# Masking whole key tiles through the bias of the exponents instead of through a matrix product

## The chip, the cores and the metric

The kernel runs on one core of a Trainium2 chip. The metric is the device time of one execution in microseconds (us), the median of three runs. A core has a matrix engine (TensorE, PE in the profile, with its weight loads shown as PEld), three engines for elementwise work (VectorE or DVE, ScalarE or ACT, GpSimd or POOL), and SyncE (SP), which here only issues DMAs. The engines run side by side, each through its own instructions in order, and wait for each other through semaphores. Products land in PSUM, everything else lies in SBUF.

## The reference

Two stages over a batch of 4 sequences of 512 tokens, 128 features each. The first stage, where the change lies, is full attention with 16 heads of 64:

```
x1 = x + attention(layernorm(x))
scores = (q @ k.T) / 8 ;  scores += -50 * (key is later than query)
out = softmax(scores) @ v ;  attention = out @ Wr
```

The mask is a penalty of -50 and no exclusion: a later key keeps its exponent, smaller by exp(-50). The second stage is six layers of local attention and feed-forward on layernorm(x1); the change does not touch it.

## The kernel before

In the first stage a piece of work is a `Rows` object: one sequence `b`, one pair of heads `c` (8 pairs) and one tile `t` of 128 queries (4 tiles), 128 pieces in all. Each does this:

- `scores` (L250): four products, two key halves of 256 for each of two heads, into a PSUM tile `sc` of 128 x 2 x 512. There are two such tiles, so a piece reuses the tile of the piece two before it.
- `penalty` (L263): for each head, a bf16 product of a 128 x 128 identity with `pen`, added onto `sc` from column t*128 to the end, which is 512, 384, 256 or 128 columns for t = 0, 1, 2, 3. `pen` holds -50 where column > row: within the query's own tile it is a triangle, and over all the tiles behind it is the constant -50.
- `maximum` (L275, VectorE): the negated maximum `nm` over all 512 keys for both heads.
- `exponents` (L281, ScalarE): one exponent per head over 512 columns, with `nm` as the bias, and the sum of the row into `den` as a by-product, which the profile shows as a second, short instruction.
- `inverse` (L290, VectorE), `normalise` (L293, GpSimd): 1/den, and its product with the whole tile `pr` of exponents (three buffers).
- `transposes` (L304): eight TensorE transposes into two PSUM banks `pt`, copied into `pT` by ScalarE for the first head (L308) and by VectorE for the second (L310).
- `times_v1` (L321), two slots later, multiplies by v; VectorE copies the result out (L331).

The order is written out by hand: no scheduler moves anything. A loop over `m` makes 64 slots of two pieces, `now[0]` and `now[1]`. **Even slots** hold the query tiles 0 and 1, **odd slots** 2 and 3. TensorE's order in a slot is: `times_v1` of an older pair, scores of both pieces, penalties of both, a product for v (`make_v`, odd slots) or a step of a layernorm (some even slots), transposes of the previous slot's first piece (`old[0]`), one of `make_q` (even) or `make_k` (odd), transposes of `old[1]`. The product bank `ps_pj` that `make_q`, `make_k`, `make_v` and the layernorms use exists once. ScalarE's order in a slot is: copy of `old[0]`, two exponents of `now[0]`, copy of q (L216, even slots), copy of `old[1]`, two exponents of `now[1]`. VectorE's is: maximum of `now[0]`, copy of v (L236, odd slots), copy of `old[0]`, maximum of `now[1]`, copy of k (L222, odd slots), inverse of `now[0]`, copy of `old[1]`, inverse of `now[1]`. A layernorm's first step puts a subtraction (L95) and a square on VectorE and ScalarE ahead of the copies, in six of the even slots; its second step includes a reciprocal root (`rsqrt`, L79 to L85), most of which runs on GpSimd.

Of the kernel before, what the change touches and what calls it, by code (L numbers as in the profile page):

```python
# [8 lines left out]
F32 = mybir.dt.float32  # L9
BF16 = mybir.dt.bfloat16  # L10
I32 = mybir.dt.int32
AF = mybir.ActivationFunctionType
ALU = mybir.AluOpType
AX = mybir.AxisListType

P = 128
# [8 lines left out]
NW = P // W  # L25
EPS = 1e-5
NEG = -1e30
NVEC = 9


@with_exitstack
def body(ctx: ExitStack, tc: tile.TileContext, a, out: bass.AP):
# [5 lines left out]
    nc = tc.nc  # L38
    x = a["x"]
    B, S, _ = x.shape  # L40
    L = a["wqkv"].shape[0]
    NT = S // P
# [5 lines left out]
    small = ctx.enter_context(tc.tile_pool(name="small", bufs=4))  # L48
# [16 lines left out]
    ident16 = const.tile([P, P], BF16, tag="ident16", name="ident16")  # L65
    vecs = const.tile([P, L, NVEC], F32, tag="vecs", name="vecs")

# [73 lines left out]
    s1 = steps[0].enter_context(tc.tile_pool(name="s1", bufs=1))  # L141
# [26 lines left out]
    with tc.manual_schedule():  # L168
# [1 line left out]
        wk = s1.tile([P, INNER], F32, tag="wk", name="wk")  # L170
        wv = s1.tile([P, INNER], F32, tag="wv", name="wv")
        wr = s1c.tile([P, NC, EMB], F32, tag="wr", name="wr")
        pen = s1.tile([P, S], BF16, tag="pen", name="pen")
        xr = [s1.tile([P, NT, EMB], F32, tag="xr", name=f"xr{b}", bufs=2) for b in range(B)]
        for b in range(B):
            nc.sync.dma_start(out=xr[b], in_=x[b].rearrange("(t p) e -> p t e", p=P))
# [10 lines left out]
        def bank1():  # L187
            return ps1b.tile([P, 512], F32, tag="pj", name="ps_pj", bufs=1)
# [23 lines left out]
        def make_q(b, c):  # L212
            p = bank1()
            mm(p, lhsT=wq[:, c * P : (c + 1) * P], rhs=xnT[b], start=True, stop=True)
            q = qs[b, c] = s1.tile([P, S], F32, tag="q1", name="q1", bufs=2)
            nc.scalar.activation(q, p, AF.Copy, scale=0.125)  # L216

        def make_k(b, c):
            p = bank1()
            mm(p, lhsT=wk[:, c * P : (c + 1) * P], rhs=xnT[b], start=True, stop=True)  # L220
            k = ks[b, c] = s1.tile([P, S], F32, tag="k1", name="k1", bufs=2)
            nc.vector.tensor_copy(k, p)  # L222

        def make_v(b, j, t):

# [12 lines left out]
        class Rows:  # L238
# [19 lines left out]

            def penalty(self):

                sc, t = self.sc, self.t
                for h in range(2):
                    mm(  # L263
                        sc[:, h, t * P : S],
                        lhsT=ident16,
                        rhs=pen[:, 0 : S - t * P],
                        start=False,
                        stop=True,
                        skip_group_check=True,
                    )  # L270

            def maximum(self):
                sc = self.sc
                self.nm = small.tile([P, 2], F32, tag="nm", name="nm")
                nc.vector.tensor_reduce(self.nm, sc, AX.X, ALU.max, negate=True)  # L275

            def exponents(self):
                self.pr = s1.tile([P, 2, S], F32, tag="pr1", name="pr1", bufs=3)
                self.den = small.tile([P, 2], F32, tag="den", name="den")
                for h in range(2):  # L280
                    nc.scalar.activation(  # L281
                        self.pr[:, h, :],
                        self.sc[:, h, :],
                        AF.Exp,
                        bias=self.nm[:, h : h + 1],
                        accum_out=self.den[:, h : h + 1],
                    )

            def inverse(self):
                nc.vector.reciprocal(self.den, self.den)  # L290

            def normalise(self):
                nc.gpsimd.tensor_tensor(  # L293
                    self.pr, self.pr, self.den.unsqueeze(2).to_broadcast([P, 2, S]), ALU.mult
                )

            def transposes(self):
                b, c, t = self.b, self.c, self.t
                if t == 0:
                    pTs[b, c] = s1b.tile([P, 2, NT, S], F32, tag="pT1", name="pT1", bufs=2)  # L300
                for h in range(2):
                    pt = pt_bank()
                    for k in range(NT):
                        nc.tensor.transpose(pt[:, k * P : (k + 1) * P], self.pr[:, h, k * P : (k + 1) * P], ident)  # L304
                    dst = pTs[b, c][:, h, :, t * P : (t + 1) * P]
                    src = pt.rearrange("p (k q) -> p k q", k=NT)
                    if h == 0:
                        nc.scalar.copy(dst, src)  # L308
                    else:
                        nc.vector.tensor_copy(dst, src)  # L310

        def times_v1(b, c, half):

# [28 lines left out]
        mean, var, scale = norm_x(0)  # L342
# [4 lines left out]
        load_x(2)  # L347
        load_x(3)
        scale()
        make_q(0, 0)  # L350
        make_k(0, 0)


        last = len(rows) // 2
        for m in range(last + 1):
            b, c, odd = m // (2 * NC), m // 2 % NC, m % 2
            now = rows[2 * m : 2 * m + 2]
            old = rows[2 * m - 2 : 2 * m] if m else []
            if m >= 4:
                g = m // 2 - 2  # L360
                times_v1(g // NC, g % NC, odd)
            for r in now:
                r.scores()
            for r in now:
                r.penalty()
            if now:
                now[0].maximum()
            if m < 2:
                make_v(0, 0, 2 * m)
                make_v(0, 0, 2 * m + 1)  # L370
            if odd and c < NT:
                make_v(b, 1, c)
            elif odd and b + 1 < B:
                make_v(b + 1, 0, c - NT)
            if not odd and 1 <= c <= 3 and b + 1 < B:
                if c == 1:
                    norms[b + 1] = norm_x(b + 1)
                norms[b + 1][c - 1]()
            if b in range(1, B) and not odd and 4 <= c <= 6:
                norms1[b - 1][c - 4]()  # L380
            if old:
                old[0].transposes()
            if now:
                now[0].exponents()
                now[1].maximum()

            bn, cn = (b, c + 1) if c + 1 < NC else (b + 1, 0)
            if bn < B:
                (make_k if odd else make_q)(bn, cn)
            if now:  # L390
                now[0].inverse()
                now[0].normalise()
            if old:
                old[1].transposes()
            if now:
                now[1].exponents()
                now[1].inverse()
                now[1].normalise()
            if b > 0 and c == 1 and odd:
                y = bank1()  # L400
                project_out1(b - 1, y)
                residual1(b - 1, y)
                norms1[b - 1] = norm_x1(bank1, b - 1)
            if b == B - 1 and c == 2 and not odd:
                start = shifted(0), layer_tables(0)
# [379 lines left out]
    def slot(n, now, last):  # L785
# [15 lines left out]
        if u:  # L801
            exponents(u)
# [53 lines left out]
    with tc.manual_schedule():  # L856
# [4 lines left out]
        for n in range(-1, len(units) + NT + 3):  # L861
            if 1 <= n < 4:
                late[n - 1]()
            q = n // NT - 1
# [4 lines left out]
def _constants(n):  # L869

    import ml_dtypes
    import numpy as np

    f = np.float32
    half = np.arange(0, HD, 2, dtype=f)
    inv_freq = (f(1.0) / np.power(f(10000.0), half / f(HD))).astype(f)
    t = np.arange(n, dtype=f)
    freqs = (t[:, None] * inv_freq[None, :]).astype(f)
    base = ((half + f(0.4 * HD)) / f(1.4 * HD)).astype(f)
    power = (t - f(n // 2)) / f(W // 2)  # L880
    scale = np.power(base[None, :], power[:, None]).astype(f)
    cos, sin = np.cos(freqs), np.sin(freqs)
    inv = (f(1.0) / scale).astype(f)
    nt = n // P

    def by_token(lo, hi):
        return np.concatenate([lo, hi], 1).astype(f).reshape(nt, P, HD).transpose(1, 0, 2)


    tabs = np.stack(  # L890
        [
            by_token(cos * scale, cos * scale) * f(8.0),
            by_token(-sin * scale, sin * scale) * f(8.0),
            by_token(cos * inv, cos * inv),
            by_token(-sin * inv, sin * inv),
        ],
        axis=2,
    )

    q = np.arange(W)[:, None]  # L900
    k = np.arange(2 * W)[None, :] - W
    seen = (q >= k) & (q <= k + W)
    band = np.zeros((P, 2, 2 * W), f)
    for r in range(0, P, HD):
        band[r : r + W, 0] = np.where(seen & (k >= 0), 0.0, NEG)
        band[r : r + W, 1] = np.where(seen, 0.0, NEG)
    band = band.astype(ml_dtypes.bfloat16)

    pen = np.where(np.arange(n)[None, :] > np.arange(P)[:, None], -50.0, 0.0).astype(ml_dtypes.bfloat16)
    ident16 = np.eye(P).astype(ml_dtypes.bfloat16)  # L910
    return {"tabs": tabs, "band": band, "pen": pen, "ident16": ident16}

# [48 lines left out]
```

## Time and profile before

| | |
|---|---|
| median of three runs | 2291.53 us (2286.24 to 2292.44) |
| the profiled execution | 2288.88 us, of which the span of instructions is 2287.1 us |
| TensorE busy over the span | 2193.9 us, 96% |
| VectorE, ScalarE, GpSimd busy | 1684.3, 1299.6, 1453.9 us |
| first stage | from about 27 us (first scores) to about 562 us |
| granted TensorE clock | 0.996 of full |

A profile line gives an instruction group by its source line (L263), engine, operation, and the tiles out<-in. A timeline line begins with the start and the duration in us; "x16" says that 16 instructions were merged, and the bracket says how long the engine stood idle before it and what ended that. The end of a matmul is modelled and includes the time in which its result drains, so the distance between the starts of two groups tells more of TensorE than its busy time.

### The profile page before, as it was taken

What the parts mean: (1) busy time and instruction counts of PE and PEld (TensorE: products, weight loads), DVE (VectorE), ACT (ScalarE), POOL (GpSimd) and SP (SyncE); (2) the same over time, 40 slices, a digit from 0 to 9 for tenths busy, and PEclk for the clock granted to TensorE, in tenths of its full rate; (3) what the DMA queues carried; (4) which work ended last, traced back from release to release, by engine and by line L of the source; (5) the groups of instructions that cost most, each with busy time, mean ns of one, the idle gap of its engine ahead of it and who ended that gap; (6) DMA issues with size and microseconds to landing.
All of it is one profiled execution on the core that took longest, in us unless ns stands there. A gap on an engine that the chain in (4) does not pass through costs nothing.

```text
span 2287.1 us, 81570 instructions
## 1 busy us (share of the span) xinstructions
PE 2193.9 (96%) x35056; PEld 1445.6 (63%) x35088; DVE 1684.3 (74%) x2608; ACT 1299.6 (57%) x2166; POOL 1453.9 (64%) x1981
## 2 busy tenths in 40 slices
PE   6999999999999999999999999999999999999997
PEld 3555555555566666666666666666666666666664
DVE  3665656655778887788887888878888878888773
ACT  2554545544445666666666656566665666666562
POOL 1544545445777676777676777677766777766760
PEclk9999999999999999999999999999999999999998
DMA  3000000000322233222322323222332223222220
GB/s 117 1 1 1 1 1 1 1 1 1 75 62 68 62 87 74 64 69 68 88 69 61 75 66 94 63 64 68 85 83 61 68 63 87 76 66 71 65 56 15
DMA packets 91025, 125.81 MB, mean 55 GB/s; under 512 B 25262, under 2 KB 39468, under 8 KB 90668
## 3 DMA queue, kind: packets, MB, share of 16 engines
q1 hardware_dynamic: 90236, 119.02, 21.0%
q8 instruction: 279, 4.57, 0.9%
q10 hardware_dynamic: 432, 1.57, 0.2%
q14 instruction: 78, 0.64, 0.1%
HBM read 20.41 MB, written 1.05 MB: 9 GB/s over the span
## 4 chain that ended last, share of the span: by engine, by line
PE 84%; DVE 11%; issue 2%; ACT 1%; DMA 1%; POOL 0%; SPq 0%; POOLq 0%; ACTq 0%; DVEq 0%
PE ps_proj L459 19%; PE ps_one L567 13%; PE ps_one L662 7%; PE ps_att L637 6%; PE ps_att L605 6%; PE ps_sc L250 5%; PE ps_o L321 5%; PE ps_pt L304 4%; PE ps_proj L695 3%; PE ps_proj L696 3%; PE ps_proj L709 2%; DVE t L484 2%; DVE rot L480 2%; DVE yt L79 2%; PE ps_sc L263 2%
## 5 line engine op out<-in xcount | busy, mean ns | idle before, releaser
L495 POOL TENSOR_TENSOR rot<-rot,t 128x1024 f32<-128x1024 f32 x192 | 454.1, 2365 | 197.9 <-DVE t L484 195.3
L459 PE MATMUL ps_proj<-wqkv,xs 128*128 128x512 f32 x1152 | 554.5, 604 | 4.8 <-DVE t L484 3.2
L293 POOL TENSOR_TENSOR pr<-pr,den 128x1024 f32<-128x1024 f32 x128 | 240.8, 1894 | 270.9 <-DVE den L290 269.6
L470 ACT ACTIVATE sq<-ps_proj 128x1024 f32<-128x1024 f32 x192 | 196.9, 1026 | 358.7 <-PE ps_proj L459 305.8
L503 POOL TENSOR_TENSOR rot<-rot,ss 128x1024 f32<-128x1024 f32 x192 | 365.5, 1904 | 14.9
L459 PEld LDWEIGHTS ps_proj<-wqkv,xs 128*128 128x128 f32 x1152 | 198.4, 190 | 167.0 <-issue 146.8
L475 DVE TENSOR_REDUCE ss<-sq 128x16 f32<-128x1024 f32 x192 | 233.2, 1215 | 47.9 <-ACT sq L470 47.2
L275 DVE TENSOR_REDUCE nm<-ps_sc 128x2 f32<-128x1024 f32 x128 | 156.1, 1220 | 122.6 <-PE ps_sc L263 122.6
L480 DVE TENSOR_TENSOR rot<-ps_proj,lt 128x1024 f32<-128x1024 f32 x192 | 233.6, 1217 | 0.0
L484 DVE TENSOR_TENSOR t<-ps_proj,lt 128x1024 f32<-128x1024 f32 x192 | 233.1, 1214 | 0.4 <-POOL rot L495 0.4
L662 PEld LDWEIGHTS ps_one<-aT,wo 128*128 128x128 f32 x1536 | 187.0, 192 | 46.9 <-issue 46.2
L567 PE MATMUL ps_one<-ident,rot 128*128 128x128 f32 x1536 | 210.5, 280 | 4.7 <-issue 2.1
L308 ACT COPY pT<-ps_pt 128x512 f32<-128x512 f32 x128 | 75.1, 587 | 235.4 <-PE ps_pt L304 233.3
L82 POOL TENSOR_TENSOR yt<-y 128x32 f32<-128x32 f32 (+1 forms) x309 | 73.5, 238 | 209.6 <-DVE y L80 193.3
L615 DVE TENSOR_REDUCE mx<-ps_att 128x16 f32<-128x1024 f32 x96 | 117.5, 1224 | 101.6 <-PE ps_att L605 99.9
L662 PE MATMUL ps_one<-aT,wo 128*128 128x128 f32 x1536 | 187.9, 275 | 1.2 <-issue 0.9
L281 ACT ACTIVATE pr<-ps_sc,nm 128x512 f32<-128x512 f32 x256 | 175.1, 696 | 9.7 <-DVE nm L275 9.7
L567 PEld LDWEIGHTS ps_one<-ident,rot 128*128 128x128 f32 x1536 | 164.5, 141 | 24.0 <-issue 4.4
L637 PEld LDWEIGHTS ps_att<-vw,pT 64*32 64x32 f32 x9216 | 103.2, 105 | 93.2 <-ACT pT L570 53.7
L549 ACT COPY vt<-ps_proj 128x512 f32<-128x512 f32 x192 | 103.2, 590 | 93.9 <-PE ps_proj L459 92.3
L304 PEld LDWEIGHTS ps_pt<-ident,pr 128*128 128x128 f32 x1024 | 118.6, 142 | 55.9 <-issue 47.4
L637 PE MATMUL ps_att<-vw,pT 64*32 64x65 f32 x9216 | 128.9, 225 | 24.1 <-DVE t L484 14.5
(132 smaller groups left out, 3996.1 us busy)
## 6 DMA issues: line engine op xcount, KB each, us to landing
vw<-vt SPq DMA_DIRECT2D x1152, 65.0 KB, 2.1
vw_first<-vt SPq DMA_DIRECT2D x336, 65.0 KB, 2.0
wqkv<-in_wqkv_dram SPq DMA_DIRECT2D x18, 512.0 KB, 7.3
wo<-in_wo_dram SPq DMA_DIRECT2D x6, 512.0 KB
w<-in_w_dram SPq DMA_DIRECT2D x6, 341.0 KB, 4.0
xr<-in_x_dram SPq DMA_DIRECT2D x4, 256.0 KB, 5.6
out_dram<-tmp_t SPq DMA_DIRECT2D x4, 256.0 KB
w<-in_w_dram SPq DMA_DIRECT2D x12, 64.0 KB, 2.9
```

The costliest lines, as they stand in the source:

```text
L293: nc.gpsimd.tensor_tensor(self.pr, self.pr, self.den.unsqueeze(2).to_broadcast([P, 2, S]), ALU.mult)
L304: nc.tensor.transpose(pt[:, k * P : (k + 1) * P], self.pr[:, h, k * P : (k + 1) * P], ident)
L459: mm(p[:, c, :], lhsT=u.xs[:, u.T * P : (u.T + 1) * P], rhs=wpart[j][:, c * 512 : (c + 1) * 512], start=True, stop=True,)
L470: nc.scalar.activation(u.sq, u.p[j], AF.Square)
L475: nc.vector.tensor_reduce(u.ss[:, j * HEADS : (j + 1) * HEADS], heads(u.sq), AX.X, ALU.add)
L480: nc.vector.tensor_tensor(heads(t0), heads(pf), lt[:, u.T, 2 * j].unsqueeze(1).to_broadcast([P, HEADS, HD]), ALU.mult)
L484: nc.vector.tensor_tensor(t1.rearrange("p (h t d) -> p h t d", t=2, d=half), pf.rearrange("p (h t d) -> p h t d", t=2, d=half)[:, :, ::-1, :],
L495: nc.gpsimd.tensor_tensor(u.r[j], u.r[j], u.t1, ALU.add)
L503: nc.gpsimd.tensor_tensor(heads(u.r[j]), heads(u.r[j]), u.ss[:, j * HEADS : (j + 1) * HEADS].unsqueeze(2).to_broadcast([P, HEADS, HD]), AL ...
L567: nc.tensor.transpose(tp[:, c * P : (c + 1) * P], src[:, (4 * g + c) * P : (4 * g + c + 1) * P], ident)
L637: mm(o[j * W : (j + 1) * W, h, c * (HD + 1) : (c + 1) * (HD + 1)], lhsT=u.pT[h * HD : (h + 1) * HD, 4 * g + c, j * W : (j + 1) * W], rhs=u ...
L662: mm(y[:, 0:P], lhsT=wo_w[0][:, c, :], rhs=u.aT[:, c, :], start=(c == 0), stop=(c == NC - 1))
```

## The change

The penalty's product covers only the query's own tile: 128 columns for each head, whatever t is. Keys behind that tile get their -50 through the bias of the exponents: the exponents of a piece are cut in two segments at column (t+1)*128, and the second uses `nm - 50`. Pieces with t = 3 have no second segment. Each segment has its own sum, so the two sums are added before the reciprocal. `maximum` now reads scores behind the own tile without their penalty, which shifts the bias of the whole row and cancels in the division. `pen` shrinks to 128 x 128. Besides, two copies on ScalarE, that of q (even slots) and that of `old[1]`, are issued after the exponents of `now[1]` instead of before them.

```diff
-                        sc[:, h, t * P : S],
+                        sc[:, h, t * P : (t + 1) * P],
                         lhsT=ident16,
-                        rhs=pen[:, 0 : S - t * P],
+                        rhs=pen,
...
-                self.nm = small.tile([P, 2], F32, tag="nm", name="nm")
-                nc.vector.tensor_reduce(self.nm, sc, AX.X, ALU.max, negate=True)
+                self.nm = small.tile([P, 2, 2], F32, tag="nm", name="nm")
+                nc.vector.tensor_reduce(self.nm[:, 0], sc, AX.X, ALU.max, negate=True)
+                if self.t + 1 < NT:
+                    nc.vector.tensor_scalar(self.nm[:, 1], self.nm[:, 0], PEN, None, ALU.add)
...
-                for h in range(2):
-                    nc.scalar.activation(
-                        self.pr[:, h, :],
-                        self.sc[:, h, :],
-                        AF.Exp,
-                        bias=self.nm[:, h : h + 1],
-                        accum_out=self.den[:, h : h + 1],
-                    )
+                seen = (self.t + 1) * P
+                for part_, cols in enumerate((slice(0, seen), slice(seen, S))):
+                    for h in range(2):
+                        if cols.start < S:
+                            nc.scalar.activation(
+                                self.pr[:, h, cols],
+                                self.sc[:, h, cols],
+                                AF.Exp,
+                                bias=self.nm[:, part_, h : h + 1],
+                                accum_out=self.den[:, part_, h : h + 1],
+                            )
 
             def inverse(self):
-                nc.vector.reciprocal(self.den, self.den)
+                if self.t + 1 < NT:
+                    nc.vector.tensor_tensor(self.den[:, 0], self.den[:, 0], self.den[:, 1], ALU.add)
+                nc.vector.reciprocal(self.den[:, 0], self.den[:, 0])
...
+            copies = []
             if bn < B:
-                (make_k if odd else make_q)(bn, cn)
+                copies.append((make_k if odd else make_q)(bn, cn))
             if now:
                 now[0].inverse()
                 now[0].normalise()
             if old:
-                old[1].transposes()
+                copies.append(old[1].transposes(later=True))
             if now:
                 now[1].exponents()
+            for f in copies:
+                f()
+            if now:
                 now[1].inverse()
                 now[1].normalise()
```

With `later=True` the transposes hand back ScalarE's copy of the first head as a function instead of issuing it; `make_q` does the same with its copy, `make_k` hands back an empty function.

More of the change, by code (lines that the diff above doesn't have):

```diff
@@ L27 @@
 NEG = -1e30
+PEN = -50.0
 NVEC = 9
@@ L172, in body @@
         wr = s1c.tile([P, NC, EMB], F32, tag="wr", name="wr")
-        pen = s1.tile([P, S], BF16, tag="pen", name="pen")
+        pen = s1.tile([P, P], BF16, tag="pen", name="pen")
         xr = [s1.tile([P, NT, EMB], F32, tag="xr", name=f"xr{b}", bufs=2) for b in range(B)]
@@ L215, in make_q @@
             q = qs[b, c] = s1.tile([P, S], F32, tag="q1", name="q1", bufs=2)
-            nc.scalar.activation(q, p, AF.Copy, scale=0.125)
+            return lambda: nc.scalar.activation(q, p, AF.Copy, scale=0.125)
         def make_k(b, c):
@@ L222, in make_k @@
             nc.vector.tensor_copy(k, p)
+            return lambda: None
         def make_v(b, j, t):
@@ L273, in maximum, with transposes @@
                 sc = self.sc
-                self.nm = small.tile([P, 2], F32, tag="nm", name="nm")
-                nc.vector.tensor_reduce(self.nm, sc, AX.X, ALU.max, negate=True)
+                self.nm = small.tile([P, 2, 2], F32, tag="nm", name="nm")
+                nc.vector.tensor_reduce(self.nm[:, 0], sc, AX.X, ALU.max, negate=True)
+                if self.t + 1 < NT:
+                    nc.vector.tensor_scalar(self.nm[:, 1], self.nm[:, 0], PEN, None, ALU.add)
             def exponents(self):
                 self.pr = s1.tile([P, 2, S], F32, tag="pr1", name="pr1", bufs=3)
-                self.den = small.tile([P, 2], F32, tag="den", name="den")
-                for h in range(2):
-                    nc.scalar.activation(
-                        self.pr[:, h, :],
-                        self.sc[:, h, :],
-                        AF.Exp,
-                        bias=self.nm[:, h : h + 1],
-                        accum_out=self.den[:, h : h + 1],
-                    )
+                self.den = small.tile([P, 2, 2], F32, tag="den", name="den")
+                seen = (self.t + 1) * P
[9 more added lines that the diff above has]
+                            )
             def inverse(self):
-                nc.vector.reciprocal(self.den, self.den)
+                if self.t + 1 < NT:
+                    nc.vector.tensor_tensor(self.den[:, 0], self.den[:, 0], self.den[:, 1], ALU.add)
+                nc.vector.reciprocal(self.den[:, 0], self.den[:, 0])
             def normalise(self):
                 nc.gpsimd.tensor_tensor(
-                    self.pr, self.pr, self.den.unsqueeze(2).to_broadcast([P, 2, S]), ALU.mult
+                    self.pr, self.pr, self.den[:, 0].unsqueeze(2).to_broadcast([P, 2, S]), ALU.mult
                 )
-            def transposes(self):
+            def transposes(self, later=False):
                 b, c, t = self.b, self.c, self.t
@@ L307, in transposes @@
                     if h == 0:
-                        nc.scalar.copy(dst, src)
+                        first = lambda dst=dst, src=src: nc.scalar.copy(dst, src)
+                        if not later:
+                            first()
                     else:
                         nc.vector.tensor_copy(dst, src)
+                return first
         def times_v1(b, c, half):
@@ L349, in body @@
         scale()
-        make_q(0, 0)
+        make_q(0, 0)()
         make_k(0, 0)
@@ L907, in _constants @@
     band = band.astype(ml_dtypes.bfloat16)
-    pen = np.where(np.arange(n)[None, :] > np.arange(P)[:, None], -50.0, 0.0).astype(ml_dtypes.bfloat16)
+    pen = np.where(np.arange(P)[None, :] > np.arange(P)[:, None], PEN, 0.0).astype(ml_dtypes.bfloat16)
     ident16 = np.eye(P).astype(ml_dtypes.bfloat16)
```

## The prediction

> **What bounds the kernel now.** I read the busy table by windows first. In the steady part of the first stage, 60 to 540 us, TensorE is busy 98% of the time and no other engine above 60%:
>
> ```profile
> core 0: us, PE busy (x) PEld busy (x) DVE busy (x) ACT busy (x) POOL busy (x), PEclk, DMA share, GB/s
> 60.00:540.00 480.00, 471.84 (x2817) 280.09 (x2847) 286.99 (x465) 239.11 (x614) 236.06 (x193) 1.00 0.00 1
> ```
>
> A busy TensorE can hide drains, so I then read starts in the timeline of TensorE, over an ordinary even slot (279.85) and the odd slot behind it (287.11):
>
> ```profile
> 279.85 2.00 PE L250 MATMUL ps_sc<-k,q 64*128 64x256 f32 x16
> 282.00 0.70 PE L263 MATMUL ps_sc<-pen,ident 128*128 128x512 bf16 x3 [0.16 <-issue]
> 282.55 1.04 PE L304 MATMUL ps_pt<-ident,pr 128*128 128x128 f32 x8
> ...
> 287.11 2.00 PE L250 MATMUL ps_sc<-k,q 64*128 64x256 f32 x16
> 289.04 0.50 PE L263 MATMUL ps_sc<-pen,ident 128*128 128x256 bf16 x4
> 289.38 1.08 PE L229 MATMUL ps_pj<-wv,xnT 128*128 128x512 f32 x2
> ...
> 295.15 2.00 PE L250 MATMUL ps_sc<-k,q 64*128 64x256 f32 x16
> ```
>
> Each group starts where the one before has streamed out; an even slot is 7.26 us, an odd one 8.04. Of the even penalties one record is missing (x3), but the weights of L263 come at 281.77 and the transposes start at 282.55. So the stage is TensorE's own work, and its nearest rival is the release of `sc` by the exponents. The timeline of the same even slot shows that chain:
>
> ```profile
> 282.42 1.23 DVE L275 TENSOR_REDUCE nm<-ps_sc 128x2 f32<-128x1024 f32 x1 [2.57 <-PE ps_sc L263]
> 283.18 0.59 ACT L308 COPY pT<-ps_pt 128x512 f32<-128x512 f32 x1 [3.60 <-PE ps_pt L304]
> 283.62 0.69 DVE L310 COPY pT<-ps_pt 128x512 f32<-128x512 f32 x1
> 283.74 0.69 ACT L281 ACTIVATE pr<-ps_sc,nm 128x512 f32<-128x512 f32 x1
> 284.23 1.21 DVE L275 TENSOR_REDUCE nm<-ps_sc 128x2 f32<-128x1024 f32 x1
> 284.42 0.68 ACT L281 ACTIVATE pr<-ps_sc,nm 128x512 f32<-128x512 f32 x1
> 285.08 0.59 ACT L216 ACTIVATE q<-ps_pj 128x512 f32<-128x512 f32 x1
> 285.56 0.59 ACT L308 COPY pT<-ps_pt 128x512 f32<-128x512 f32 x1
> 286.03 0.72 ACT L281 ACTIVATE pr<-ps_sc,nm 128x512 f32<-128x512 f32 x1
> 286.70 0.71 ACT L281 ACTIVATE pr<-ps_sc,nm 128x512 f32<-128x512 f32 x1
> ```
>
> The last exponent ends at 287.41. The next slot's second piece needs its tile .97 after that slot's start (half of the 1.93 us of the 16 score products), at 288.08. Where TensorE really stood (start of the stage) it resumed .14 after an exponent's end (38.31 + .69, next 39.14). The slack is thus .53 us. In odd slots it is 1.18; in the six even slots with a layernorm's first step it is nothing (exponent ends .14 before the product).
>
> **What the Trainium skill says.** *TensorE: Matmul & The Clock Gate*, "Wait — 56ns, not 53.3ns?": back-to-back products start 55.6 ns apart at 128 columns, 215.7 at 512. The trace agrees: 56 ns between the last two starts of an odd penalty group, 216 between 512-wide ones. Its section "Back-to-back issue gap" gives 81 ns for pairs of weight load and 128-wide product; no run here shows that. *ScalarE: Activation LUTs*, "What ACT_TABLE_LOAD costs": an ACTIVATE with a pointer bias takes about 280 ns + .833 ns per column. The trace gives 693 at 512 against 707. *GPSIMD Engine Reference*, "Specifications": GpSimd shares its SBUF interfaces with VectorE instructions in a two-port mode or with two SBUF inputs. The trace agrees: L79, a tiny VectorE operation on SBUF, lasts 170 ns or until the GpSimd operation beside it ends.
>
> ```profile
> L79 DVE TENSOR_SCALAR yt<-rs x32: 170/1324/1862, 12.8 to 2263.5; 128x4 int32<-128x4 int32 x32
> ```
>
> **Part 1, the narrower penalty, on the path.** Even: 2 x 216 + 2 x 162 = 756 ns (1,792 columns) becomes 4 x 56 = 224; saved .53 us. Odd: .34 (289.04 to 289.38) becomes .224; saved .115. No product is removed, 256 stay. Bounds: at 81 ns a pair the saving is .43 and .015. I take 56, from this trace. At most 32 x (.53 + .115) = 20.6 us.
>
> **Part 2, 192 more exponents on ScalarE (8 instead of 4 in an even slot, 6 instead of 4 in an odd).** Each also issues a 208 ns sum read. In the trace a 512-wide exponent starts .675 after the one before, its duration less about .015, so the read hides. From the page's 280 + .833N I estimate durations of 387, 493 and 600 ns for 128, 256 and 384 columns, and intervals of .37, .48 and .585. A split of 512 then costs .28 more per head, 192 x .28 = 54 us of ScalarE, which has 241 us free in the window; what counts is the chain. Upper bound: the read does not hide and each interval is .2 longer. Lower: the trace's .675 less .833 ns per column, .355 at 128 columns; I keep both for the range.
>
> **Part 3, small VectorE operations: 96 `nm - 50`, 96 additions of sums.** A dependent one costs about .2 (L79 to L80 start .22 apart), an independent copy starts .09 behind it. So `nm - 50` adds about .13 behind a maximum. It is queued ahead of the copy of `old[0]` and of the second maximum, which row 1's exponents await. The addition delays the reciprocal and GpSimd's product by .2. Both read SBUF, so either can sit out a 1.89 us product on GpSimd.
>
> **The chain after, ordinary even slot**, from the slot's start. The first maximum waits for two 56 ns products instead of two of 216: 2.57 becomes 2.25, ending 3.48. `nm - 50` starts at 3.52, the copy at 3.60 (3.77 before), the second maximum .61 later, ending 5.43 (5.59). ScalarE's first exponent, before at 3.89, starts at 3.55; two intervals of .37 and two of .585 bring it to 5.46. Copies of q and `old[1]` no longer stand between. Row 1 starts at 5.50 and ends three intervals of .48 and .49 later: 7.43 (7.56 before). The next slot now starts at 7.26 - .53 = 6.73 and wants the tile at 7.70; free at 7.43 + .14 = 7.57. Margin .13: TensorE stays the bound, barely.
>
> **Odd slots**: row 1 (t = 3) is not split and ends near 7.6, wanted at 8.9. No loss. **Six layernorm slots**: the square delays row 0 to 5.25, row 1 to 7.16, end 9.09 + .14 = 9.23, wanted at 8.33 - .53 + .97 = 8.77. TensorE waits .46, so .07 of .53 is left. **First slot**: TensorE takes 1.39 us for its penalties (30.89 to 32.28), and the chain decides; earlier maxima and the q copy moved back, less longer exponents, give about .8. **End of the stage**: TensorE waits for the last GpSimd products anyway (idle .75 us before L304 at 559.79); addition and split delay them by .65.
>
> **The moved copies** are costed at nothing. The q copy now ends about 8.0 in an even slot; `ps_pj` is next needed by `make_v` at 6.73 + 2.16 = 8.9. The `old[1]` copy ends by 8.5; its bank is next needed after 9.3. If that cover went, the next transposes would be late. **GpSimd**: an even slot's first product runs 6.2 to 8.1, so the second addition (wanted 7.63) is held to 8.1 and the second product ends near 10.4, 3.65 into the odd slot, where the transposes want it after 11.8 - 6.7 = 5.1. There it holds `nm - 50` by .15; the odd slot's slack covers that. An odd slot's last product ends 3.10 into the next even slot, .42 before `nm - 50` wants to run. The smaller `pen` DMA lies in the load phase and ends nothing.
>
> **Sum**: 25 ordinary even slots x .53 = 13.3; 6 x .07 = .4; first .8; 31 odd x .115 = 3.6; end -.65: 17.4 us, against the profiled execution's 2288.9 us (span 2287.1, 1.8 around it): 2271.5. The median of the runs is 2.6 above that execution, which gives 2274. I predict 2272.
>
> **Rivals.**
> A. The margin of .13 is overrun: `nm - 50` is held by GpSimd in even slots too, or intervals are a few hundredths longer. Each .3 per even slot costs 7.5 us. For: .42 and .13 are small. Against: slots repeat to .01 us. Gain 7 to 14, 2279; chance .13.
> B. Slower. The sum read of short exponents does not hide. Place: ScalarE's eight exponents of an even slot; price .2 each. Row 0 then takes 2.75 instead of 1.91 and row 1 ends near 9.05, where 7.56 would do: a wait of 1.5, a net loss of 1.0. In 25 slots that is 24, in the six layernorm slots 1.5 each, less 3.6 in odd ones: about +30, 2319. It decides from .08 per exponent, where (.13 + .53) / 8 is used up. Against: the read hides at 512. Chance .06.
> C. Weight loads pace the small products at 81 ns: about 25 x .43 + .5 + 1.2 = 12 us gained, 2277. Against: 56 ns in the trace. Chance .05.
> D. The change doesn't save what it says: the chain, not TensorE, already sets even slots, so .53 goes into a wait and only some odd ones remain: within 3 us of no change, 2289. For: the six slots without slack. Against: .53 of slack elsewhere. Chance .06.
>
> **Numbers.** The forecast has .70: gain 14 to 20, 2268 to 2275, with 3 us of run spread either way 2265 to 2278. A range of 2264 to 2281 adds C and most of A and leaves out B and D. Faster by over .3% (7 us, about what a measurement of this kernel can tell from no change) gathers the forecast, C and nearly all of A: .87; within .3% .07; slower .06.
>
> **What would show it.** Right: penalty groups of .22 us, ordinary even slots of about 6.73, odd near 7.92, layernorm slots near 8.25 and now waiting for L290's exponents, ScalarE some 54 us busier. Wrong: intervals between exponents above .46 at 128 columns or .57 at 256, `nm - 50` longer than .2 us in even slots, or TensorE idle before ordinary slots' scores.

## The result and the profile after

The changed kernel takes 2284.22 us (median, 2281.46 to 2287.14) against 2288.46 for the kernel before (2285.14 to 2292.71), 15 runs each. The ratio is 0.9975, 95% interval 0.9969 to 0.9982: faster, but by 6 us and not by 17. The profiled execution took 2281.5 us, its span is 2279.7.

Line numbers have moved: scores are L252, the penalty L267, the maximum L279, `nm - 50` L281, the copy of v L238, `make_k` L221, `make_q` L215, the addition of the sums L300, the exponents L290. First the busy table by windows of the changed kernel, over the same 480 us:

```profile
60.00:540.00 480.00, 465.31 (x2883) 275.25 (x2883) 332.14 (x648) 287.21 (x976) 237.61 (x194) 1.00 0.00 1
```

ScalarE is 48 us busier and VectorE 45, as the added instructions would have it (time in which GpSimd holds them included), but TensorE has lost 6.5 us of its busy time to idling. Where, the timeline shows for a plain even slot (127.50) and the odd slot behind it (134.28). TensorE first:

```profile
127.50 2.00 PE L252 MATMUL ps_sc<-k,q 64*128 64x256 f32 x16
129.43 0.40 PE L267 MATMUL ps_sc<-pen,ident 128*128 128x128 bf16 x4
129.66 1.04 PE L315 MATMUL ps_pt<-ident,pr 128*128 128x128 f32 x8
...
134.28 2.00 PE L252 MATMUL ps_sc<-k,q 64*128 64x256 f32 x16
136.21 0.40 PE L267 MATMUL ps_sc<-pen,ident 128*128 128x128 bf16 x4
136.44 1.08 PE L231 MATMUL ps_pj<-wv,xnT 128*128 128x512 f32 x2
137.36 1.04 PE L315 MATMUL ps_pt<-ident,pr 128*128 128x128 f32 x8
138.61 1.13 PE L221 MATMUL ps_pj<-xnT,wk 128*128 128x512 f32 x2 [0.21 <-DVE v L238]
139.57 1.04 PE L315 MATMUL ps_pt<-ident,pr 128*128 128x128 f32 x8
140.54 1.94 PE L335 MATMUL ps_o<-pT,v 128*64 128x512 f32 x8
142.41 0.49 PE L252 MATMUL ps_sc<-k,q 64*128 64x256 f32 x2
```

The penalties take .23 us in both slots, and the even slot shrank to 6.78. The odd slot is 8.12, longer than before: TensorE stands before `make_k` (L221), and the bracket names the copy of v. VectorE's lines of the same slot tell why:

```profile
136.53 1.23 DVE L279 TENSOR_REDUCE nm<-ps_sc 128x2 f32<-128x1024 f32 x1 [0.20 <-PE ps_sc L267]
137.79 0.17 DVE L281 TENSOR_SCALAR nm<-nm 128x2 f32<-128x2 f32 x1
137.87 0.69 DVE L238 COPY v<-ps_pj 128x512 f32<-128x512 f32 x1
```

The maximum starts .11 earlier in its slot than before, `nm - 50` takes its place in the queue, and the copy of v, which empties the only `ps_pj`, ends at 138.55. `make_k` starts .06 behind that. From the maximum's start to the copy's start it is now 1.34 us. The kernel before shows the same order without `nm - 50`, in the odd slot that begins at 287.11:

```profile
289.47 1.22 DVE L275 TENSOR_REDUCE nm<-ps_sc 128x2 f32<-128x1024 f32 x1 [1.12 <-PE ps_sc L263]
290.62 0.68 DVE L236 COPY v<-ps_pj 128x512 f32<-128x512 f32 x1
291.35 0.30 PEld L220 LDWEIGHTS ps_pj<-xnT,wk 128*128 128x128 f32 x2 [0.25 <-DVE v L236]
```

There it was 1.15 from the maximum to the copy, and there too `make_k` started .05 behind the end of the copy. So the odd slots before look as if they were not TensorE's own work either, which e9 tests below. The view of waits (engine and line, what it waited for: us, times, longest) names the same copy, first before, then after:

```profile
PEld ps_pj L220 <- DVE v L236: 6.8, 27, 0.3
```

```profile
PEld ps_pj L221 <- DVE v L238: 14.9, 27, 0.8
PE ps_pj L221 <- DVE v L238: 8.5, 27, 0.6
PE ps_pj L215 <- DVE xnT L115: 2.1, 3, 0.7
PE ps_pj L215 <- DVE xT L115: 2.1, 3, 0.7
PE ps_pj L215 <- DVE tmp_t L96: 1.1, 5, 0.2
```

The last three are the same wait in the even slots with a layernorm's first (L96) or third step (L115): `make_q` awaits a bank that VectorE empties behind `nm - 50`.

### The profile page after: what moved, and what is told of

Same layout as the page of the kernel before. It is cut to its first block, busy times and chain, and to the rows that moved or that the text cites. A ratio compares the mean times of both kernels' runs of the same rounds, so it can differ in the third digit from the quotient of the medians.

```text
span 2279.7 us, 82205 instructions
## 1 busy us (share of the span) xinstructions
PE 2178.0 (96%) x35088; PEld 1435.6 (63%) x35088; DVE 1729.1 (76%) x2800; ACT 1347.6 (59%) x2550; POOL 1451.3 (64%) x1981
## 4 chain that ended last, share of the span: by engine, by line
PE 63%; DVE 9%; issue 2%; ACT 1%; POOL 0%; POOLq 0%; ACTq 0%
PE ps_proj L477 19%; PE ps_one L585 14%; PE ps_one L680 7%; PE ps_att L655 6%; PE ps_att L623 6%; PE ps_proj L713 3%; PE ps_proj L714 3%; PE ps_proj L727 2%; DVE yt L80 2%; DVE t L502 1%; DVE rot L498 1%; PE ps_att L612 1%; PE ps_one L94 1%; PE ps_one L103 1%; DVE yt L83 1%
## 5 line engine op out<-in xcount | busy, mean ns | idle before, releaser
L290 ACT ACTIVATE pr<-ps_sc,nm 128x128 f32<-128x128 f32 (+3 forms) x448 | 220.1, 507 | 20.0 <-DVE nm L279 16.7
L279 DVE TENSOR_REDUCE nm<-ps_sc 128x2 f32<-128x1024 f32 x128 | 156.0, 1219 | 91.0 <-PE ps_sc L267 91.0
```

The costliest lines, as they stand in the source:

```text
L290: nc.scalar.activation(self.pr[:, h, cols], self.sc[:, h, cols], AF.Exp, bias=self.nm[:, part_, h : h + 1], accum_out=self.den[:, part_, h ...
```

## The experiments

**The theory**: what the narrow penalty gains is real, and `nm - 50`, which stands on VectorE ahead of the operation that empties `ps_pj`, takes it back. **The rival**: the 192 more exponents on ScalarE take it back. The table holds mean slot lengths in us, from one trace each: the distance between the first score products of two neighbouring slots. "Odd" is the mean of the same 14 slots in every row. Left out are four more of their kind: two that were longer already before the change, and two of 8.34 and 8.29 in the changed kernel, where GpSimd held `nm - 50` (it lasted .39 and .33). A single late slot raises three of the means (8.63 in e3, 8.47 in e7, 7.01 among the plain even ones of e6); the others of the row stand at 8.23, 8.12 and 6.78. "Sum" is from the first slot's scores to the last slot's. The last column is the measured ratio to the kernel before, with its interval. Each ratio is to runs of the kernel before made beside it (medians 2288.46 for the changed kernel, 2285.50 for e1 to e4, 2285.71 for e5 to e8, 2290.49 for e9), so ratios are to be compared, not the medians given below.

| kernel | plain even | layernorm step 1 | step 3 | odd | odd behind step 2 | sum | ratio |
|---|---|---|---|---|---|---|---|
| before | 7.27 | 8.33 | 8.24 | 8.03 | 8.03 | 525.2 | |
| changed | 6.78 | 8.12 | 8.12 | 8.12 | 8.47 | 519.2 | .9975 (.9969 to .9982) |
| e1_shift_behind | 6.78 | 7.92 | 7.92 | 7.93 | 7.93 | 508.6 | .9934 (.9913 to .9956) |
| e2_narrow_alone | 6.74 | 7.92 | 7.92 | 7.93 | 7.93 | 507.0 | .9909 (.9884 to .9933) |
| e3_before_nm50 | 7.27 | 8.44 | 8.44 | 8.26 | 8.23 | 534.1 | 1.0043 (1.0028 to 1.0059) |
| e4_split_alone | 7.27 | 8.33 | 8.24 | 8.03 | 8.03 | 525.0 | 1.0006 (.9994 to 1.0018) |
| e5_copies_back | 6.78 | 8.12 | 8.12 | 8.58 | 8.60 | 535.2 | 1.0057 (1.0041 to 1.0073) |
| e6_v_on_scalar | 6.80 | 8.12 | 8.12 | 7.71 | 7.72 | 507.0 | .9938 (.9917 to .9958) |
| e7_sum_by_reduce | 6.78 | 8.12 | 8.12 | 8.15 | 8.12 | 516.4 | .9971 (.9960 to .9982) |
| e8_all_three | 6.78 | 7.92 | 7.92 | 7.72 | 7.71 | 503.1 | .9910 (.9893 to .9928) |
| e9_before_v_scalar | 7.27 | 8.33 | 8.24 | 7.82 | 7.82 | 519.8 | .9978 (.9970 to .9985) |

**e1_shift_behind: only the place of `nm - 50`.**

```diff
                 nc.vector.tensor_reduce(self.nm[:, 0], sc, AX.X, ALU.max, negate=True)
+
+            def shift(self):
                 if self.t + 1 < NT:
                     nc.vector.tensor_scalar(self.nm[:, 1], self.nm[:, 0], PEN, None, ALU.add)
...
                 norms1[b - 1][c - 4]()
+            if now:
+                now[0].shift()
             if old:
...
                 now[1].maximum()
+                now[1].shift()
```

> The changed kernel with one move: nm - 50 of a slot's first piece is issued behind the copy of v (odd slots) or the layernorm's step (even slots) instead of ahead of it. Theory (the product bank ps_pj is held longer because nm - 50 stands ahead of VectorE's copy out of it, and make_k or make_q waits for that bank): the copy of v starts .14 to .2 earlier, ordinary odd slots go from 8.12 to about 7.97, odd slots behind a layernorm's second step from 8.47 to about 8.15, the twelve even slots with a layernorm's first or third step from 8.12 to about 7.93; in all 6 to 8 us faster than the changed kernel, ratio to before about .9945. Rival (the longer exponents on ScalarE cost the gain): slots stay at 8.12 and 8.47, ratio .9975.

Measured: 2271.21 us. Every slot that had been blamed on the bank shrank to where the theory had it or below, with the same instructions on every engine as in the changed kernel. In an odd slot the copy of v now starts 1.14 behind the maximum's start, much as in the kernel before (1.15). `make_k` still waits for that copy (135.90 to 135.96), only it ends earlier:

```profile
134.08 1.23 DVE L279 TENSOR_REDUCE nm<-ps_sc 128x2 f32<-128x1024 f32 x1 [0.20 <-PE ps_sc L267]
135.22 0.68 DVE L238 COPY v<-ps_pj 128x512 f32<-128x512 f32 x1
135.82 0.16 DVE L283 TENSOR_SCALAR nm<-nm 128x2 f32<-128x2 f32 x1
135.96 1.12 PE L221 MATMUL ps_pj<-xnT,wk 128*128 128x512 f32 x2
```

All 192 added exponents are still there, so the rival falls by this alone.

**e2_narrow_alone: the gain alone.** The edit is the narrow `pen` and the narrow product in the kernel before, nothing else; keys behind the query's own tile get no penalty at all.

```diff
-                        sc[:, h, t * P : S],
+                        sc[:, h, t * P : (t + 1) * P],
                         lhsT=ident16,
-                        rhs=pen[:, 0 : S - t * P],
+                        rhs=pen,
```

> The kernel before with the narrow penalty alone: 128 columns for every t; the -50 on the tiles behind the query's own is left out, so nothing is split, added or moved. Theory: plain even slots 7.26 to 6.74, even slots with a layernorm's first or third step lose only what the first maximum comes earlier (.32), odd slots gain .11 to .12 (8.03 to 7.92), since make_k waits for the copy of v behind the maximum; in all about 15 us faster than before, ratio .9935. Rival (the change's missing gain lies in the penalty itself, as at 81 ns a product): even slots near 6.9, odd slots unchanged, under 11 us.

Measured: 2265.79 us, 18.2 us less in the sum of the slots. Both part sizes of the prediction are there, .53 in plain even slots and .11 in odd ones (.115 predicted). Slots with a layernorm's step gain less even here: .41, .48 and .32 for the first, second and third step. In the steady part e1 has all of it but .04 per plain even slot; what those .04 are was not followed.

**e3_before_nm50: the suspected cost alone**, in the kernel before.

```diff
+                self.nm2 = small.tile([P, 2], F32, tag="nm2", name="nm2")
                 nc.vector.tensor_reduce(self.nm, sc, AX.X, ALU.max, negate=True)
+                if self.t + 1 < NT:
+                    nc.vector.tensor_scalar(self.nm2, self.nm, -50.0, None, ALU.add)
```

> The kernel before with one thing added: a VectorE operation nm2 = nm - 50 of 128 x 2 behind each maximum with t below 3, whose result nobody reads. Theory: it stands ahead of the copy out of ps_pj, so every odd slot with a make_v grows by about .2 (8.03 to 8.23), even slots with a layernorm's first or third step by about .2, plain even slots by nothing; in all 7 to 9 us slower, ratio 1.003 to 1.004. Rival (ScalarE): the operation is hidden, no slot grows, ratio 1.000.

Measured: 2295.00 us. An operation of 128 x 2 elements that nobody reads costs 9 us in the sum of the slots. In its timeline, VectorE's operation, the copy of v and `make_k`:

```profile
295.87 0.17 DVE L278 TENSOR_SCALAR nm<-nm 128x2 f32<-128x2 f32 x1
295.95 0.68 DVE L236 COPY v<-ps_pj 128x512 f32<-128x512 f32 x1
296.69 1.13 PE L220 MATMUL ps_pj<-xnT,wk 128*128 128x512 f32 x2 [0.21 <-DVE v L236]
```

The bracket before TensorE's product is the one of the changed kernel, .21.

**e4_split_alone: the rival's cost alone.** The changed kernel with the wide penalty and no `nm - 50`.

```diff
-                if self.t + 1 < NT:
-                    nc.vector.tensor_scalar(self.nm[:, 1], self.nm[:, 0], PEN, None, ALU.add)
...
-                                bias=self.nm[:, part_, h : h + 1],
+                                bias=self.nm[:, 0, h : h + 1],
...
-                        sc[:, h, t * P : (t + 1) * P],
+                        sc[:, h, t * P : S],
...
-                        rhs=pen,
+                        rhs=pen[:, 0 : S - t * P],
```

> The changed kernel with the wide penalty of before and no nm - 50: exponents are split, both segments with the same bias, sums are added, the two copies on ScalarE stand behind the exponents. So ScalarE's share of the change alone. Theory: no slot is more than .05 longer than before save those odd slots behind a layernorm's second step, where GpSimd holds the addition (up to .2); in all 0 to 2 us slower, ratio 1.000 to 1.001. Rival (the longer exponents cost the gain): odd slots at least .2 longer, 7 us or more slower, ratio 1.003.

Measured: 2286.54 us, no slot of the steady part longer. ScalarE carries 280.07 us in the window instead of 239.11 and no slot grows by it. The .2 that I had kept for GpSimd's hold did not show, though additions were held there too and lasted up to .91 us. This run alone would not settle the rival, since its even slots are half a microsecond longer than those of the changed kernel; e1 does.

**e5_copies_back: the moved copies.** They go back in front of the second piece's exponents.

```diff
-                copies.append((make_k if odd else make_q)(bn, cn))
+                (make_k if odd else make_q)(bn, cn)()
...
-                copies.append(old[1].transposes(later=True))
+                old[1].transposes()
...
-            for f in copies:
-                f()
```

> The changed kernel with the copies of q and of old[1] on ScalarE back in front of the second piece's exponents, as before the change. Theory: in a plain even slot row 1's exponents start after 5.46 + .5 + .46 = 6.4 and end near 8.35, .14 more and the tile is free at 8.5, wanted at 7.70; plain even slots grow from 6.78 to about 7.5 and the whole is some 12 to 18 us slower than the changed kernel, ratio to before 1.003 to 1.006. Rival (the copies' place doesn't matter, ps_pj is all there is): slots as in the changed kernel, ratio .9975.

Measured: 2299.94 us, as expected in sum. The place I had wrong: the plain even slot keeps its 6.78, and the wait stands inside the next slot, before the second piece's scores. The 8.58 in the table mixes two kinds: odd slots behind a plain even slot grew to 8.84, those behind a third step stayed at 8.12.

```profile
138.47 1.13 PE L252 MATMUL ps_sc<-k,q 64*128 64x256 f32 x8
140.05 1.13 PE L252 MATMUL ps_sc<-k,q 64*128 64x256 f32 x8 [0.44 <-ACT pr L290]
```

The second half starts 1.58 behind the first, not .97. So moving the copies is what makes room for the longer exponents; with them in their old place the change is slower than the kernel before. Both were put back together, so what each is worth is not shown.

**e6_v_on_scalar: another way out of the same queue.**

```diff
-            nc.vector.tensor_copy(vs[b, j][:, t, :], p)
+            (nc.scalar.copy if act else nc.vector.tensor_copy)(vs[b, j][:, t, :], p)
...
-                make_v(b, 1, c)
+                make_v(b, 1, c, m > 1)
...
-                make_v(b + 1, 0, c - NT)
+                make_v(b + 1, 0, c - NT, True)
```

> The changed kernel with one edit: the copy of v in the odd slots from the second on runs on ScalarE, which stands idle there, instead of on VectorE behind the maximum and nm - 50. Theory: make_k no longer waits, odd slots become TensorE's own work, 8.12 and 8.47 to about 7.75; 27 slots, in all 9 to 12 us faster than the changed kernel, ratio to before about .993. Rival (ScalarE's load costs the gain): one more copy on ScalarE delays the exponents, odd slots 8.12 or longer, ratio .9975 or above.

Measured: 2272.79 us. TensorE's timeline of an odd slot now runs from the transposes into `make_k` without a stop:

```profile
135.16 1.04 PE L315 MATMUL ps_pt<-ident,pr 128*128 128x128 f32 x8
136.03 1.09 PE L221 MATMUL ps_pj<-xnT,wk 128*128 128x512 f32 x2
```

.87 from group to group, against 1.25 in the changed kernel. ScalarE took one more copy per odd slot and the stage got faster, against the rival.

**e7_sum_by_reduce: the shared interface.** In the changed kernel odd slots behind a layernorm's second step lose .35 more than others. There GpSimd is late, and VectorE's operations sit out its products (POOL):

```profile
203.65 1.89 POOL L304 TENSOR_TENSOR pr<-pr,den 128x1024 f32<-128x1024 f32 x1
204.30 1.26 DVE L300 TENSOR_TENSOR den<-den 128x2 f32<-128x2 f32 x1 [0.92 <-ACT pr L290]
205.59 0.17 DVE L301 RECIPROCAL den<-den 128x2 f32<-128x2 f32 x1
205.67 0.67 DVE L345 COPY aT<-ps_o 128x512 f32<-128x512 f32 x1
205.93 1.89 POOL L304 TENSOR_TENSOR pr<-pr,den 128x1024 f32<-128x1024 f32 x1 [0.39 <-DVE den L301]
206.26 1.22 DVE L279 TENSOR_REDUCE nm<-ps_sc 128x2 f32<-128x1024 f32 x1
207.51 0.33 DVE L281 TENSOR_SCALAR nm<-nm 128x2 f32<-128x2 f32 x1
207.76 0.68 DVE L238 COPY v<-ps_pj 128x512 f32<-128x512 f32 x1
```

The slot starts at 203.82. The addition lasts until the first product is over, so the maximum starts 2.44 into the slot instead of 2.25. That shifts GpSimd's second product too, and now `nm - 50` is held until it is over: .33 instead of .17. The .19 and the .16 are the .35. The edit, after which the reciprocal and GpSimd's product read `inv`:

```diff
...
-                    nc.vector.tensor_tensor(self.den[:, 0], self.den[:, 0], self.den[:, 1], ALU.add)
+                    self.inv = small.tile([P, 2], F32, tag="inv", name="inv")
+                    nc.vector.tensor_reduce(self.inv, self.den.rearrange("p a h -> p h a"), AX.X, ALU.add)
...
```

> The changed kernel with the addition of the two sums done by a VectorE reduction over one input instead of a tensor_tensor with two inputs in SBUF. Reductions over SBUF were not held by GpSimd in the traces. Theory: the operation no longer sits out GpSimd's product (up to 1.27 us in the changed kernel, now about .17 each), so in the odd slots behind a layernorm's second step the copy of the result and the first maximum come earlier: 8.47 to about 8.2; ordinary odd slots stay at 8.12; in all 1 to 3 us faster than the changed kernel, ratio about .9967. Rival (GpSimd's hold costs nothing): slots as in the changed kernel.

Measured: 2279.44 us. By the ratio it can't be told from the changed kernel; the slots tell it, in one trace but in five slots alike: 8.47 became 8.12. The hold costs this only in company: e1 keeps the addition, which lasts 1.09 us in the same slot, and has 7.93 there, with `nm - 50` out of the way. The addition's durations (least, median, longest ns), in the changed kernel and here:

```profile
L300 DVE TENSOR_TENSOR den<-den x96: 145/161/1269, 36.3 to 551.8; 128x2 f32<-128x2 f32 x96
```

```profile
L302 DVE TENSOR_REDUCE inv<-den x96: 140/156/159, 36.5 to 549.2; 128x2 f32<-128x4 f32 x96
```

**e8_all_three: e1, e6 and e7 together.**

> The changed kernel with all three edits: nm - 50 behind the layernorm's step and the copy of v, that copy on ScalarE, the sums added by a reduction. Theory: odd slots 7.75, even slots with a layernorm's first or third step 7.93, plain even slots 6.78: about 14 us faster than the changed kernel, near 2270, ratio to before .9915. If ScalarE were the bound, no better than the changed kernel.

Measured: 2266.23 us, faster than both kernels, and by the ratio not to be told from e2, which leaves work out. What is left of the wait are the layernorm slots, 7.92, where `make_q` still follows VectorE's operation.

**e9_before_v_scalar: was the stage before TensorE's own work?** The edit of e6, in the kernel before.

> The kernel before with one edit: the copy of v in the odd slots from the second on runs on ScalarE instead of VectorE; penalty, exponents and order otherwise untouched. Theory (make_k already waited for the product bank ps_pj before the change): its product starts .18 earlier, odd slots 8.03 to about 7.85, even slots unchanged; in all about 5 us faster than before, ratio .998. Rival (the stage before was TensorE's own work throughout, as the prediction had it): no slot is shorter, ratio 1.000.

Measured: 2285.36 us against 2290.49, and odd slots of 7.82. The kernel before already lost .21 per odd slot to the bank, with TensorE shown as busy.

## Why the prediction was wrong

- **The part that was right.** Products of 128 columns follow each other at 56 ns; the penalty group takes .23. Plain even slots went to 6.78, .48 less each (predicted .53, which e2 shows in full); those with a second step went to 7.63, .48 less in e2 as well. The chain to the release of `sc` holds. These are ScalarE's exponents in the changed kernel, two each of 256, 384 and 128 columns:

```profile
133.93 0.47 ACT L290 ACTIVATE pr<-ps_sc,nm 128x256 f32<-128x256 f32 x1
134.38 0.48 ACT L290 ACTIVATE pr<-ps_sc,nm 128x256 f32<-128x256 f32 x1
138.48 0.59 ACT L290 ACTIVATE pr<-ps_sc,nm 128x384 f32<-128x384 f32 x1
139.04 0.58 ACT L290 ACTIVATE pr<-ps_sc,nm 128x384 f32<-128x384 f32 x1
139.60 0.38 ACT L290 ACTIVATE pr<-ps_sc,nm 128x128 f32<-128x128 f32 x1
139.94 0.38 ACT L290 ACTIVATE pr<-ps_sc,nm 128x128 f32<-128x128 f32 x1
```

The last exponent of the slot at 127.50 ends at 134.86, .58 into the next slot, .14 more is .72, wanted at .97. The margin of .13 was really .25: .07 because the exponents are a little quicker than estimated (intervals of .34, .45 and .56 for .37, .48 and .585), and .05 because the slot is 6.78 and not 6.73. The sum read hides (rival B falls), weight loads don't pace the products (C), and the moved copies do what was reckoned (e5). The first slot gained .75 (.8 predicted), and from the last slot's scores to the stage's last transposes it takes .6 longer (.65 predicted); no run takes these two apart.
- **The step that failed**: "Odd slots: ... No loss", entered as a gain of 31 x .115 = 3.6 us. From the third odd slot to the second to last they grew by 4.9 us: 14 x .09, 5 x .44, and ten others. Part 3 named the copy of `old[0]` and the second maximum as queued behind `nm - 50`, and left out the copy of v, which in odd slots stands first. The place of `make_k` behind it was never tested: the paragraph on the moved copies followed `ps_pj` from `make_q` to `make_v` and stopped there. A size was off besides. Part 3 priced `nm - 50` at .13 behind a maximum; it is .19 (1.34 less 1.15). Less the .11 by which the maximum comes earlier that is .08, about the .09 that was measured. With .13 the two would nearly have cancelled, so the omitted wait explains why there was no gain, and the missing .06 most of the loss in ordinary slots.
- **The same omission in even slots**: the six with a third step were counted as ordinary at .53 and saved .12 (2.5 us missing in sum). Those with a first step were priced at .07 by a wait for the exponents; five saved .21, bounded by `ps_pj` and not by `sc` (e1: 7.92), and the sixth, the third slot of all, lost .63. Their sum of .4 is as predicted by luck. Of the 12 us that are missing in all (17.4 forecast; the slots gave 6.0, less .6 at the end), odd slots make 8.3 and third steps 2.5.
- **"So the stage is TensorE's own work" was too strong.** The .25 before L220 in the view of waits looked like the usual gap of a weight load. `make_k`, which started .05 behind another engine's copy, was waiting for it, whatever the busy column says; e9 puts .21 per odd slot on it.
- **GpSimd's hold** was seen, for `nm - 50` with .15 and for the addition, and placed in the slack of odd slots. The size was right where it came up (.16 for `nm - 50` behind a second step), the slack was not: it belonged to `sc`, and the queue runs to `ps_pj` (e7: .35 in each of five such slots by the trace).
- **Rivals and signs.** The gain lies between rival D (within 3 us) and rival A (7 to 14), nearer to A; but A put the overrun into even slots, and in plain even slots `nm - 50` was never held. D's wait was in the wrong place. To a change within .3% the prediction gave .07. In the steady part none of its three signs of being wrong came up: they looked at the exponents, at even slots and at the scores, none at `ps_pj`.
- **Open.** The third slot grew by .63 in the changed kernel, by .45 with the split alone, and by .08 in e1. With `nm - 50` moved it is nearly gone, yet the split without `nm - 50` has most of it: the parts are not separated.

## What to carry to other kernels

A tiny operation is priced by what stands behind it in its queue, so list every instruction behind it up to the next point where another engine waits, and for each ask which buffer it frees. A buffer with one copy deserves that question first. Whether an engine is the bound is read from what ended just before each of its groups starts, not from its busy share.

## What the runs showed of the hardware

The page *GPSIMD Engine Reference*, "Specifications", says that GpSimd contends with VectorE instructions in a two-port mode or with two SBUF inputs. The addition of the sums has two, and agrees: 33 of its 96 in the changed kernel lasted over .25 us, up to 1.27. The reduction over the same sums has one: in e7 33 of 96 started while GpSimd was at work, and none lasted more than .16. That makes it a way around. One input alone is no safeguard, though: `nm - 50` has one and was held too, in 16 of 96 cases, up to .52 us; whether that is the page's two-port mode no run here shows.

Splitting an exponent costs ScalarE a third more: two heads of 128 + 384 columns take 2 x (.34 + .56) = 1.80 us by the intervals, against 2 x .675 = 1.35 unsplit. With the two copies moved, the slots of e1 in the steady part are no longer than those of e2, which splits nothing, save .04 in a plain even slot.
